# Moving thirty small on-chip DMAs from SyncE's queue to ScalarE's, behind the copy that feeds them

## The chip, the cores and the metric

The kernel runs on one core of a Trainium2 chip. A core has a matrix engine (TensorE, PE in the profile), a vector engine (VectorE, DVE), an activation engine (ScalarE, ACT), a general engine (GpSimd, POOL) and a synchronisation engine (SyncE, SP). Each works through its own list of instructions in order and waits on semaphores. DMAs are issued by an engine's instruction and carried out by 16 DMA engines. The metric is the device time of one execution in microseconds (us).

## The reference

The input x is 2 batches of 1024 tokens of width 512. Cut to what is computed:

```
xn = layernorm(x)                              # no gain, no bias
q, k, v = (xn @ W.T + b for W, b in ...)       # 32 heads of 16 values each
att = softmax(causal(q @ k.T / 4))
s   = (att @ v) @ Wo.T + bo
g   = silu(xn @ Wb.T + bb + routed low-rank delta of 8 experts, best 2)
out = x + s * g
```

Everything is float32.

## The kernel before, in words

**Units and steps.** The attention is cut into 16 units (b, oc, c): a batch b of 2, a group oc of 8 heads (4 groups), and a chunk c of 512 query tokens (2 chunks). A unit is a row of steps: 5 steps for c = 0 and 13 for c = 1 (`unit_steps`, from L1199). The plan has 144 steps. In step n TensorE makes the scores of a 128-key block against up to 512 queries for 4 heads, two of them to a score tile (`scores`, L1524, matmuls at L1538), ScalarE takes the exponential of them in two instructions, one for each score tile (`pt<-s`), GpSimd zeroes what the causal mask forbids (`masked`, L1553, L1566 in the profile; only in steps on the diagonal), and TensorE multiplies with the values (`values`, L1571, matmuls at L1590). TensorE's order is: scores of step n, values of step n - 1, then filling work of step n, then scores of step n + 1. The filling work are the projections (`q`, `p`, `pq`, `pk`, `pv`, `ph`, `po`, all matmuls at L228).

There are two score tiles a step and two buffers, so the scores of step n + 1 overwrite what the exponentials of step n read. They cannot start before these are done.

**The queries' tile.** For each unit after the first, the queries are split into a high part in a short float format (float32r) and the remainder, the low part, and both are laid out for the scores. The tile `qT` holds 128 rows and 4 planes of 512 queries. Planes 0 and 1 serve the even heads (high, low), planes 2 and 3 the odd heads. The steps are these:
- `split_queries` (L473): ScalarE writes the high part to planes 0 and 2 in one instruction (`qT<-qf`, 128x1024), VectorE subtracts and writes the low part to plane 1.
- `copy_remainder` (L478): ScalarE copies plane 1 to plane 3 (`qT<-qT`, 128x512).
- `place_queries` (L481, the DMA at L484): two DMAs inside the tile. The first copies, in planes 0 and 1, the even rows onto the odd rows; the second copies, in planes 2 and 3, the odd rows onto the even rows. Each moves 64 rows of 4096 bytes, 256 KB. Scores of the unit may start when the DMA of their planes has landed.

The keys go the same way with `place_keys` (L465), two DMAs of 128 KB for a unit.

**Who calls it.** Two units get their queries from `qk_task` (L410), the other 13 from `split` (L486). In `qk_task` the copy comes with the last but one block of the keys' projection, in `split` it is the function `remainder`, which the planner places. That makes 15 copies and 30 placing DMAs. Before the change the DMAs are issued by SyncE, whose queue also carries nearly every other transfer of the kernel: weights, x, the parts of the weights kept in DRAM, the layout change of x, the softmax denominators and the outputs.

**The planner.** All engines' orders are written out by hand (`manual_schedule`); no scheduler reorders them. A function `fill` (L1431) decides, step by step while the program is built, which small pieces come next. It keeps a guess of when VectorE and ScalarE are free (`Metered`, L40: a base price and a rate for each instruction, added to `.free`). Pieces for which a price is given in `costs` wait for a step where ScalarE has room:

```
calm = lambda more: act.free + more < begins + 0.75
...
if x[1] in costs and not calm(costs[x[1]][0]) and n < costs[x[1]][1]:
    continue
```

The first number of `costs` is the price and the second the step by which the piece goes in anyway. For `remainder` this is 3 steps ahead of the unit's first. The list `later` holds pieces for a later step, and `urgent` those that are issued at the end of a step or just ahead of the next scores (`place_urgent`, L1519).

**Semaphores of DMAs.** The program's DMAs take eight completion semaphores in turn, in the order of the program, whichever engine issues them. A DMA waits until the one that had its semaphore before it has landed.

The function that the change touches:

Of the kernel before, what the change touches and what calls it, by code (L numbers as in the profile page):

```python
# [81 lines left out]
def direct(ctx, tc, sound, x, wq, wk, wv, wo, wb, wa, wg, wB, bq, bk, bv, bo, bb, out):  # L82
# [9 lines left out]
    nc = tc.nc  # L92
    ve = Metered(nc.vector, 0.19, 966)
    act = Metered(nc.scalar, 0.22, 1274)
# [124 lines left out]
    turned_at, now = {}, [0]  # L219
    xns, xnTs, kTs, qTs, vs, gs, oTs, kfs = {}, {}, {}, {}, {}, {}, {}, []  # L220

    def mm_tile(name):
        return ps_mm.tile([P, D], F32, tag="mm", name=name)

    def matmul(o, lhsT, rhs, start, stop):

        for j in range(0, P, 32):
            nc.tensor.matmul(  # L228
                o[j : j + 32],
                lhsT=lhsT[:, j : j + 32] if len(lhsT.shape) == 2 else lhsT[:, j // 32],  # L230
                rhs=rhs,
                start=start,
                stop=stop,
            )
# [175 lines left out]
    def qk_task(b, oc, c):  # L410

        xnT = xnTs[b, c]
        qk_begun.append((b, oc, c))
        qT, kT = split_tiles(b, oc, c)
        qf = sb.tile([P, C], F32, tag="qf", bufs=2, name=f"qf_{b}_{oc}_{c}")
        kf = sb.tile([P, C], F32, tag="kf", bufs=2, name=f"kf_{b}_{oc}_{c}")
        bias_q, bias_k = (b_pair[:, n + oc : n + oc + 1] for n in (0, KC))
        pq = mm_tile("pq")
        for k in range(KC):
            matmul(  # L420
                pq, lhsT=wqks[oc][:, k, :], rhs=xnT[:, k, :], start=k == 0, stop=k == KC - 1
            )
            if k < KC - 1:
                yield MM
        act.activation(qf, pq, AF.Identity, bias=bias_q)
        split_queries(qT, qf)
        yield MM
        pk = mm_tile("pk")
        for k in range(KC):
            matmul(  # L430
                pk, lhsT=wqks[oc][:, KC + k, :], rhs=xnT[:, k, :], start=k == 0, stop=k == KC - 1
            )
            if k == KC - 2:
                copy_remainder(qT)
                later.append((now[0], lambda: place_queries(qT)))
            if k < KC - 1:
                yield MM
        if c:
            act.activation(
                kT, pk.unsqueeze(1).to_broadcast([P, 2, C]), AF.Identity, bias=bias_k  # L440
            )
            ve.tensor_scalar(kf, pk, bias_k, None, ALU.add)
            ve.tensor_tensor(kf, kf, kT[:, 0].bitcast(F32), ALU.subtract)
        else:
            act.activation(kf, pk, AF.Identity, bias=bias_k)
            split_keys(kT, kf, kf)
        later.append((now[0], lambda: place_keys(kT, kf)))
        qk_done[b, oc, c] = now[0]
        yield MM
# [8 lines left out]
    def split_keys(kT, kf, low):  # L458

        act.activation(kT, kf.unsqueeze(1).to_broadcast([P, 2, C]), AF.Copy)  # L460
        ve.tensor_tensor(low, kf, kT[:, 0].bitcast(F32), ALU.subtract)

    def place_keys(kT, low):
        for par in range(2):
            nc.sync.dma_start(out=kT[1 - par :: 2, par].bitcast(F32), in_=low[par::2])  # L465

    def split_tiles(b, oc, c):
        qT = sb.tile([P, 4, C], F32R, tag="qT", bufs=2, name=f"qT_{b}_{oc}_{c}")
        kT = sb.tile([P, 2, C], F32R, tag="kT", bufs=4, name=f"kT_{b}_{oc}_{c}")
        qTs[b, oc, c], kTs[b, oc, c] = qT, kT  # L470
        return qT, kT

    def split_queries(qT, qf):  # L473
        high = qT.rearrange("p (a h) c -> p a h c", a=2)[:, :, 0]
        act.activation(high, qf.unsqueeze(1).to_broadcast([P, 2, C]), AF.Copy)
        ve.tensor_tensor(qT[:, 1], qf, qT[:, 0].bitcast(F32), ALU.subtract)

    def copy_remainder(qT):  # L478
        act.activation(qT[:, 3], qT[:, 1].bitcast(F32), AF.Copy)

    def place_queries(qT):  # L481
        for par in range(2):
            both = qT[:, 2 * par : 2 * par + 2].bitcast(F32)
            nc.sync.dma_start(out=both[1 - par :: 2], in_=both[par::2])  # L484

    def split(b, oc, c, qf, kf):  # L486

        qT, kT = split_tiles(b, oc, c)
        split_keys(kT, kf, kf)

        def queries():
            split_queries(qT, qf)
            room["acc"] += 1
            later.append((now[0] + 1, remainder))

        def remainder():
            copy_remainder(qT)
            urgent.append((now[0], lambda: place_queries(qT)))

        by = starts[b, oc, c]  # L500
        costs[queries], costs[remainder] = (1.1, by - 4), (0.6, by - 3)
        later.append((now[0] + 1, queries))
        urgent.append((now[0] + 1, lambda: place_keys(kT, kf)))

# [264 lines left out]
    def qk_blocks_task(k):  # L769
# [36 lines left out]
        yield MM  # L806
        add(q[1], product("q4", at(1, 1)), q[1], less)
        splits.append((now[0] + 1, lambda: split(b, oc, c, qf, kf), (b, oc, c)))
        qk_done[b, oc, c] = now[0]
        ended[0] += 1  # L810
# [277 lines left out]
    turns, turned, posts, posted, later, patient, last_out = [], [], {}, [], [], [], []  # L1088
# [16 lines left out]
    bases, whole_wo, splits, costs, urgent = {}, [], [], {}, []  # L1105
# [200 lines left out]
    for b in range(NB):  # L1306
        for c in range(NC):
# [11 lines left out]
            for oc in range(KC):  # L1319
                takes = {"acc": 1}  # L1320
                if (b, oc, c) in units[1:3]:
                    Task(
                        starts[b, oc, c] - (1 if c else 2), qk_task(b, oc, c), 8 * MM, takes=takes | {"qT": 1, "kT": 1}, uses=xn, frees=takes,
                        ready=lambda u=units[units.index((b, oc, c)) - 1], t=turned_: u in qk_begun
                        and t() and (u == units[0] or now[0] >= starts[units[1]]),
                    )
                elif oc or b or c:
                    stage(
                        qk_blocks_task, ("qk", b, c, oc), starts[b, oc, c] - 5, 7 * MM, takes, xn,
                        turned_,  # L1330
                    )
# [39 lines left out]
            if (b, c) != (NB - 1, NC - 1):  # L1371
                by = min(len(plan) - 3, done + (21 if c else 22 if b else 30))
# [738 lines left out]
```

## Time and profile before

| What | Value |
|---|---|
| Time, median of 3 runs (lowest, highest) | 561.15 us (560.59, 562.68) |
| The profiled execution: its own time / its span | 560.8 us / 559.1 us |
| Granted clock of TensorE, mean | 0.993 |
| Busy: PE / DVE / ACT / POOL | 97% / 60% / 63% / 21% of the span |
| Exponentials `pt<-s` on ACT | 288, 1024 ns each, 290.2 us |
| The copies `qT<-qT` on ACT | 15, 623 ns each, 9.3 us |
| The placing DMAs on SP's queue | 30, 585 ns median each to issue |

How to read it. Busy time counts instructions that do arithmetic; a DMA's issue and a wait are not busy. An engine written with a q (SPq, ACTq) is the engine's sequencer issuing a DMA. An arrow in brackets after an idle time names what ended that idle time. A row of the timeline has the start, the duration, the engine, the line and the operation with output and input tiles; x2 means two instructions merged into one row.

### The profile page before, as it was taken

Reading aid. Unit: us, or ns where it says so; the run is one execution under the profiler, and the core shown is the slowest. Engines: PE = TensorE matmul, PEld = TensorE weight load, DVE = VectorE, ACT = ScalarE, POOL = GpSimd, SP = SyncE. Lnnn points to the kernel's source line nnn. Section 1 sums busy time; section 2 is a strip of 40 time slices with the busy share of each in tenths; the row PEclk is TensorE's granted clock in tenths of the full one; section 3 lists DMA queues with packets and bytes.
Section 4 is the critical chain, followed back from the end, with each engine's and each line's share of the span. In section 5 each row is a group of like instructions: output and inputs, shape, how many; then the busy total and the mean of one; then the engine's idle time right before and its main releaser. Section 6 shows DMA issues by size and latency. Waiting matters only on the chain.

```text
span 559.1 us, 19432 instructions
## 1 busy us (share of the span) xinstructions
PE 540.1 (97%) x8411; PEld 279.9 (50%) x8411; DVE 334.4 (60%) x693; ACT 351.5 (63%) x389; POOL 118.6 (21%) x248
## 2 busy tenths in 40 slices
PE   8999999789999999999999999999999999999994
PEld 7435444444445554454645554444545554456651
DVE  4435587266478676466559765575267553648833
ACT  2537754566677766766667756656667777776540
POOL 2213401020213431130214330130103331020500
PEclk9999999899999999999999999999999999999998
DMA  8634370686623663832555545640124221652211
GB/s 257 178 111 165 126 230 4 201 289 201 169 82 135 228 219 110 245 99 79 174 173 176 171 155 169 198 152 23 59 80 137 79 83 45 229 170 81 97 40 46
DMA packets 65198, 79.16 MB, mean 142 GB/s; under 512 B 9560, under 2 KB 52576, under 8 KB 63696
## 3 DMA queue, kind: packets, MB, share of 16 engines
q1 hardware_dynamic: 65088, 77.83, 43.4%
q8 instruction: 68, 1.11, 0.9%
q14 instruction: 26, 0.21, 0.1%
q10 hardware_dynamic: 16, 0.00, 0.0%
HBM read 46.39 MB, written 19.37 MB: 118 GB/s over the span
## 4 chain that ended last, share of the span: by engine, by line
PE 87%; DMA 5%; DVE 3%; SPq 1%; ACT 1%; issue 1%; ACTq 0%; DVEq 0%
PE av L1590 24%; PE p L228 21%; PE s L1538 17%; PE q L228 13%; PE pv L228 2%; PE po L228 2%; PE ph L228 2%; PE pq L228 1%; PE pk L228 1%; DMA qT<-qT 1%; ACT pt L56 1%; DMA back<-rc 1%; DVE x L56 1%; DMA wqk<-in_wq_dram 1%; DMA wqk<-in_wk_dram 1%; DMA gr<-kept_g 1%
## 5 line engine op out<-in xcount | busy, mean ns | idle before, releaser
L56 ACT ACTIVATE pt<-s 128x1024 f32<-128x1024 f32 x288 | 290.2, 1024 | 157.4 <-PE s L1538 149.8
L1566 POOL TENSOR_SCALAR_AFFINE_SELECT pt<-pt 128x256 f32<-128x256 f32 (+1 forms) x224 | 110.6, 509 | 414.6 <-ACT pt L56 414.0
L1590 PE MATMUL av<-pt,v 128*32 128x512 f32 (+3 forms) x1680 | 157.3, 469 | 0.2 <-DVE v L56 0.2
L1538 PE MATMUL s<-qT,kT 32*128 32x512 f32 (+3 forms) x1616 | 108.9, 364 | 6.3 <-ACT pt L56 3.8
L1538 PEld LDWEIGHTS s<-qT,kT 32*128 32x128 f32 x1616 | 62.3, 183 | 65.4 <-issue 38.7
L1590 PEld LDWEIGHTS av<-pt,v 128*32 128x32 f32 x1680 | 41.8, 109 | 54.3 <-issue 38.1
L228 PE MATMUL p<-wt,asum 128*32 128x256 f32 x960 | 58.7, 379 | 0.0
L228 PE MATMUL q<-asum,wqk 128*32 128x256 f32 x832 | 51.2, 379 | 1.7 <-DVE qf L56 1.7
L228 PEld LDWEIGHTS p<-wt,asum 128*32 128x32 f32 x960 | 31.3, 110 | 28.9 <-issue 11.7
L228 PEld LDWEIGHTS q<-asum,wqk 128*32 128x32 f32 x832 | 26.5, 110 | 26.1 <-issue 6.9
L228 PE MATMUL q<-xnT,wqk 128*32 128x256 f32 x624 | 39.5, 379 | 0.0
L56 DVE TENSOR_TENSOR g<-p,g 128x512 f32<-128x512 f32 x20 | 13.8, 689 | 26.5 <-PE p L228 26.4
L228 PEld LDWEIGHTS q<-xnT,wqk 128*32 128x32 f32 x624 | 20.2, 110 | 18.4 <-issue 6.6
L56 DVE SCALAR_TENSOR_TENSOR kf<-q,kf 128x256 f32<-128x256 f32 x39 | 16.5, 424 | 19.5 <-PE q L228 18.6
L228 PE MATMUL p<-w,xnT 128*32 128x256 f32 x448 | 28.1, 379 | 0.0
L228 PEld LDWEIGHTS p<-w,xnT 128*32 128x32 f32 x448 | 15.7, 110 | 10.3 <-issue 3.6
L228 PE MATMUL p<-w,asum 128*32 128x256 f32 x320 | 20.7, 379 | 0.0
L228 PEld LDWEIGHTS ph<-wag_sb,xnT 128*32 128x32 f32 x512 | 15.9, 114 | 4.8 <-issue 3.0
L56 DVE TENSOR_TENSOR kf<-kf,kT 128x512 f32<-128x512 f32 x15 | 10.3, 684 | 12.1 <-ACT kT L56 12.0
L228 PE MATMUL ph<-wag_sb,xnT 128*32 128x136 f32 x512 | 17.4, 287 | 0.0
L228 PE MATMUL po<-wo,oT 128*32 128x512 f32 x128 | 16.5, 593 | 0.4 <-ACT oT L56 0.4
L56 DVE TENSOR_TENSOR qT<-qf,qT 128x512 fp32r<-128x512 f32 x15 | 10.5, 699 | 10.4 <-ACT qT L56 10.4
(145 smaller groups left out, 556.3 us busy)
## 6 DMA issues: line engine op xcount, KB each, us to landing
wt<-kept SPq DMA_DIRECT2D x40, 256.0 KB
qT<-qT SPq DMA_DIRECT2D x30, 256.0 KB
x<-in_x_dram SPq DMA_DIRECT2D x16, 256.0 KB
kept<-wqk SPq DMA_DIRECT2D x4, 1024.0 KB
wqk<-kept SPq DMA_DIRECT2D x4, 1024.0 KB
kT<-kf SPq DMA_DIRECT2D x30, 128.0 KB
scr<-sq SPq DMA_DIRECT2D x6, 512.0 KB
xnT<-scr SPq DMA_DIRECT2D x24, 128.0 KB
```

Source lines behind the costliest of these rows:

```text
L56: return getattr(self.engine, name)(*args, **named)
L228: nc.tensor.matmul(o[j : j + 32], lhsT=lhsT[:, j : j + 32] if len(lhsT.shape) == 2 else lhsT[:, j // 32], rhs=rhs, start=start, stop=stop,)
L1538: nc.tensor.matmul(ss[s // 2][:, s % 2, col : col + w], lhsT=keys[rows, kt % TT * P : kt % TT * P + P], rhs=q[rows, halves * par + half_, ...
L1566: nc.gpsimd.affine_select(out=d, in_=d, compare_op=ALU.is_ge, fill=0.0, base=0, pattern=[[0, d.shape[1]], [1, P]], channel_multiplier=-1,)
L1590: nc.tensor.matmul(avs_now[par][32 * s : 32 * s + 32, q0 : q0 + w], lhsT=vs[b, kt][:, h * VS - HD * par : h * VS - HD * par + HP], rhs=pt[ ...
```

## The change

The two placing DMAs are issued by ScalarE in place of SyncE, directly behind ScalarE's copy of the remainder, in both callers. They no longer go through `later` or `urgent`. The planner's guess of ScalarE's free time is raised by 0.55 for each of the two DMAs, and the price of `remainder` goes from 0.6 to 1.7. Its last step stays the same.

```diff
             if k == KC - 2:
                 copy_remainder(qT)
-                later.append((now[0], lambda: place_queries(qT)))
+                place_queries(qT)
...
     def place_queries(qT):
         for par in range(2):
             both = qT[:, 2 * par : 2 * par + 2].bitcast(F32)
-            nc.sync.dma_start(out=both[1 - par :: 2], in_=both[par::2])
+            nc.scalar.dma_start(out=both[1 - par :: 2], in_=both[par::2])
+            act.free = max(act.free, act.ready) + 0.55
...
         def remainder():
             copy_remainder(qT)
-            urgent.append((now[0], lambda: place_queries(qT)))
+            place_queries(qT)

         by = starts[b, oc, c]
-        costs[queries], costs[remainder] = (1.1, by - 4), (0.6, by - 3)
+        costs[queries], costs[remainder] = (1.1, by - 4), (1.7, by - 3)
```

## The prediction, on record before the changed kernel had run

> **What bounds the kernel now.** I began with the page: is there an engine without idle time?
>
> ```profile
> PE 540.1 (97%) x8411; PEld 279.9 (50%) x8411; DVE 334.4 (60%) x693; ACT 351.5 (63%) x389; POOL 118.6 (21%) x248
> ```
>
> TensorE is busy for 540.1 of 559.1 us. The change adds no matmul, and the changed program has all 11459 instructions of TensorE in the old order. So it can only act through TensorE's 19 us of idle time: the first 2.5 us, some 9 us at the tail, and a few stalls between. TensorE's own waits name those that a score matmul suffers (columns: total us, times, longest):
>
> ```profile
> PE s L1538 <- ACT pt L56: 3.8, 3, 2.8
> PE s L1538 <- DMA qT<-qT: 2.3, 1, 2.3
> ```
>
> One placement of thirty stalls TensorE, for 2.3 us. That is the most this part can give. The groups show how much room ScalarE has:
>
> ```profile
> L56 ACT ACTIVATE pt<-s 128x1024 f32<-128x1024 f32 x288 | 290.2, 1024 | 157.4 <-PE s L1538 149.8
> ```
>
> Of 157.4 us idle ahead of the exponentials, 149.8 end with TensorE's scores. ScalarE normally waits for TensorE, not the reverse. What an issue costs a sequencer, SyncE's placements first (minimum, median, maximum ns), then the only two DMAs that ScalarE issues now:
>
> ```profile
> L484 SPq DMA_DIRECT2D qT<-qT x30: 464/585/1354, 39.3 to 493.8; - x30
> ```
>
> ```profile
> L152 ACTq DMA_DIRECT2D b_rows<-in_bq_dram x1: 550/550/550, 0.8 to 0.8; - x1
> L153 ACTq DMA_DIRECT2D b_rows<-in_bk_dram x1: 259/259/259, 1.4 to 1.4; - x1
> ```
>
> Then the timeline around all 15 copies. The common place, ScalarE alone:
>
> ```profile
> 163.09 0.62 ACT L56 ACTIVATE qT<-qT 128x512 fp32r<-128x512 f32 x1
> 164.63 2.02 ACT L56 ACTIVATE pt<-s 128x1024 f32<-128x1024 f32 x2 [0.91 <-PE s L1538]
> ```
>
> The copy ends at 163.72 and the next exponentials start 0.91 us later. The first of the tight places:
>
> ```profile
> 38.65 0.63 ACT L56 ACTIVATE qT<-qT 128x512 fp32r<-128x512 f32 x1 [0.76 <-DVE qT L56]
> ...
> 41.23 1.92 ACT L56 ACTIVATE pt<-s 128x1024 f32<-128x1024 f32 x2
> ...
> 43.21 1.15 PE L1538 MATMUL s<-qT,kf 32*128 32x256 f32 x16
> ```
>
> Here no idle time stands before the exponentials, and the scores start 0.05 us after these end. The last place is the tightest: copy and exponentials follow without a gap, and TensorE is already waiting for ScalarE:
>
> ```profile
> 493.13 1.92 ACT L56 ACTIVATE pt<-s 128x1024 f32<-128x1024 f32 x2
> 493.25 1.11 SPq L484 DMA_DIRECT2D qT<-qT  x2
> ...
> 495.10 0.74 PE L1538 MATMUL s<-qT,kT 32*128 32x256 f32 x14 [0.53 <-ACT pt L56]
> ```
>
> And the one stall that a placement makes:
>
> ```profile
> 118.87 6.50 DMA qT<-qT
> 125.37 0.14 issue
> 125.51 0.74 PE s L1538 x6
> ```
>
> These are pieces of the chain that ended last. The copy was done at 115.87; SyncE came to the placement 3.0 us later, behind weight loads, and it landed 6.5 us after that.
>
> [...] the pair issued from 118.87 took its sequencer 1.86 us, its first half 6.50 us to land. [...] SyncE would save 30 x 0.585 = 17.6 us, but SyncE isn't the bound. [...]
>
> **The change part by part.** *ScalarE's new work.* The first DMA waits for ScalarE's own copy, 0.03 us (SyncE starts 0.03 after a copy ends). The pair takes 1.10 to 1.19 us on SyncE where undisturbed; I take 1.15. With 0.07 to the next activation, ScalarE is ready 1.25 us after the copy's end. Bounds for the pair: 0.55 (twice ScalarE's cheaper issue) and 2.5 (twice SyncE's dearest, nearly).
>
> *What is queued behind it* is the next exponential, and behind that TensorE's next scores, which need the score tiles free. At 38.65 the key activations stand between: they start at 40.53, not 39.55, and the exponentials end at 44.14, not 43.16. TensorE loses 0.95. At 492.61 the exponentials start at 494.47, not 493.13: lost 1.3, all of it, since TensorE already waits. At 434.62 (ScalarE did a tanh just before) idle is 0.40: late by 0.85, against 0.51 from the exponentials' end to the scores; lost 0.4, and 0.1 more at the mask behind. At 451.21 late by 0.33 against 0.08: lost 0.3. Sum 3.05.
>
> At the common place it is late by 0.34: 1.25 less 0.91. Scores follow the exponentials' end by 0.53, so these hide it; the masked tiles that the values read are finished 0.38 ahead (167.48 against 167.86), so about nothing is left. Nine places like this I price at 0.4 together. Two (305.50, 354.99) have 1.6 to 1.8 us and cost nothing.
>
> *SyncE's issues in the same moment.* In five common places SyncE itself issues then (at 180.88, 197.20, 288.82, 324.24, 416.06). [...] half an issue more each time, with no cover left: 0.2 x 4, 0.8 in sum. Nothing to 3 are the bounds.
>
> *Waits for semaphores.* Each DMA on ScalarE now also waits for the one that last had its completion semaphore. I looked up all thirty in the old trace: each had landed by then, the nearest at 197.11 against 198.39 (a store of the layout change). Cost nothing; the cover is 1.3 us there, and everything beyond goes to the exponentials.
>
> *Copies moved.* The dearer price pushes five copies 1 to 7 steps later, to 2 steps ahead of their unit. From there some 7 us pass until the first scores; an undisturbed pair lands in 2.9 (163.74 to 166.67). Hidden, with 4 us left. The copy of weights `wqk` near 46 goes one step later; idle time covers it. SyncE's later transfers come 1.2 us sooner, and no TensorE stall waits for one.
>
> *The gain.* At 115.9 the placement no longer waits for SyncE. What is late next is ScalarE: its copy of `wqk` waited 2.01 us for a weight load, ran from 120.74, and the exponentials behind it ended at 123.85. Scores cannot start before 123.9: at most 1.6 of 2.34 is won. And the placement now moves 512 KB while that load is under way, 1.25 us at the 410 GB/s of 120 to 122; the engines were 0.74, 0.92 and 0.50 busy from 115 to 118, so about half of it fits: load late by 0.6[...]. Gain 0.9, bounds 0 and 2.3.
>
> *Sum.* 3.05 + 0.4 + 0.8 - 0.9 = 3.35 on the profiled execution: span 562.4, its own time 560.8 + 3.35 = 564.15. The median of the runs is 561.15, 0.35 above that execution. I say 564.3, which is 0.56% over the median. A measurement of this kernel can tell about 0.5% from no change, that is 558.3 and 564.0.
>
> **The rivals.** *Main case*, as above: chance 0.45, own range 562.8 to 566, about 0.27 of it above 564.0.
>
> *Hidden for the most part*: the pair costs ScalarE 0.8 us. Then 0.6 + 0.95 + 0.15 are lost and the rest is covered; less a gain of 1.0, 561.85. For it: 149.8 us of waiting for TensorE, and 0.26 for ScalarE's second issue. Against it: that issue moved 4 rows, these move 64, and SyncE needs 0.59 for each second one. Chance 0.27.
>
> *Not slower*: [...] the pair takes 0.55, so only 0.35 and 0.7 are lost: 559.9. It decides from where the pair's price falls under 0.95, at which the two losses are about the gain. Against it: the exponentials that end at 123.85. Chance 0.12, 0.04 of it below 558.3.
>
> *ScalarE held by the shared machinery*: [...] With the cover spent, eleven places pay in full, 5.5: 568 with a smaller gain. For it: SyncE's issues reach 1.35 and 1.43 us in the crowded stretch at 115 to 122. Against it: outside that they keep under 0.6. Chance 0.16.
>
> **How the numbers follow.** Slower: 0.27 + 0.16 = 0.43. Same: 0.18 + 0.27 + 0.08 = 0.53. Faster: 0.04. The range 560.9 to 567.5 leaves out most of the third case (0.08) and the upper part of the fourth (0.10).
>
> **What would show it.** Right: thirty issues on ACTq of 0.5 to 0.6 us, ScalarE's wait for scores down by some 17 us, TensorE waiting for `pt` some 3 us longer with entries near 44, 436 and 496, and no wait for `qT<-qT`. The stall at 123 to 125 shrinks to 1 to 2 us and is then put down to ScalarE. Wrong: issues of 0.3 us on ACTq, a step after a copy without lateness, a placement that stalls TensorE elsewhere, or ScalarE waiting for a DMA ahead of an issue.

## The result

| | before | after |
|---|---|---|
| Median (lowest to highest) | 561.83 us (560.59 to 562.68), 4 runs | 568.04 us (566.49 to 572.07), 4 runs |
| After / before | | 1.0129, 95% interval 1.0085 to 1.0174 |
| Profiled execution: span, mean clock | 559.1 us, 0.993 | 566.5 us, 0.991 |

The change makes the kernel 1.3% slower by the ratio; the medians are 6.2 us apart. 3.35 us were forecast. When both were run again it was 567.2 us against 560.49, ratio 1.0109 (1.0067 to 1.0151). A ratio in this document need not be the quotient of the medians beside it.

First the page, TensorE's row:

```profile
PE 545.7 (96%) x8411; PEld 285.2 (50%) x8411; DVE 334.6 (59%) x693; ACT 350.4 (62%) x389; POOL 117.7 (21%) x248
```

No matmul was added and TensorE is busy 5.6 us longer. The prediction had said that the change can act only through idle time. Two things make busy time grow: a lower clock (below), and ends of matmuls that the profile models, so that a matmul held up half way looks long (the step that is 0.97 us late at 44 shows only 0.21 us of waiting, below). TensorE's waits alone therefore don't give the loss:

```profile
PE s L1539 <- ACT pt L56: 6.5, 8, 2.2
PE q L228 <- DVE qf L56: 3.9, 2, 3.3
```

They were 3.8 for ScalarE and 1.7 for VectorE; the 2.3 us for `qT<-qT` is gone. ScalarE's side, the exponentials and the issues:

```profile
L56 ACT ACTIVATE pt<-s 128x1024 f32<-128x1024 f32 x288 | 289.2, 1024 | 162.9 <-PE s L1539 150.9
```

```profile
L484 ACTq DMA_DIRECT2D qT<-qT x30: 472/572/1089, 39.7 to 499.1; - x30
```

An issue on ScalarE's queue costs what it cost SyncE: median 572 ns against 585. Yet the idle time ahead of the exponentials did not fall by 17 us, it is 150.9 after 149.8. The idle column counts the issue as idle time, so it doesn't show how much of a wait a sequencer's work has used up.

A better ruler than waits, since TensorE's order is the same in both: the end of each step's second exponential, after minus before, from the two traces. Below this is called the lateness. It moves in few places (stretches of steps that move it by less than 0.02 us have no row):

| Where (steps) | changed, first profile | changed, second | queue alone |
|---|---|---|---|
| Start, before the first placement | 0.41 | 0.17 | 0.15 |
| 3 (copy at 39) | 0.97 | 0.96 | 0.97 |
| 4 to 17 | 0.11 | 0.15 | 0.01 |
| 18 to 25 (the stall at 123) | 0.42 | -0.49 | -0.86 |
| 33 to 36 (copy at 165) | 0.62 | 0.86 | 0.66 |
| 37 to 94 | 0.05 | 1.27 | 0.60 |
| 95 | 2.08 | 3.42 | -1.14 |
| 111 to 115 (copy at 439) | 0.41 | 0.42 | 0.41 |
| 116 to 128 (copy at 456) | 0.26 | 0.24 | 0.24 |
| 129 (copy at 498) | 1.31 | 1.32 | 1.32 |
| 130, 131 | 1.24 | 1.21 | 1.38 |
| 132 to 143 | 0.17 | 0.21 | -0.01 |
| Sum, and the tail behind it | 8.05, -0.62 | 9.71, -0.41 | 3.73, -0.51 |

The last column is an experiment below. In the first two, sum and tail give the spans' differences, 7.4 and 9.3 us. How good is the ruler? A second profile of the kernel before differs from the first by at most 0.07 us in every row but one: at steps 18 to 25 it is 1.98 us later. In that row lie the stall at 123 and, in the kernel before, a stretch at half clock (107 to 111), so single profiles don't give its size.

The tight places look as forecast; here is the first, in the timeline (start, duration, engine):

```profile
39.72 1.17 ACTq L484 DMA_DIRECT2D qT<-qT  x2
...
42.62 1.92 ACT L56 ACTIVATE pt<-s 128x1024 f32<-128x1024 f32 x2
...
44.59 0.50 PE L1539 MATMUL s<-qT,kf 32*128 32x256 f32 x4 [0.21 <-ACT pt L56]
```

Issue, key activations and exponentials follow one another, the exponentials start at 42.62 where they started at 41.23 (0.41 us of that arose before the copy), and TensorE waits for them.

Three losses have no term in the prediction's sum. The first stands behind the tightest place, in the timeline:

```profile
498.58 1.12 ACTq L484 DMA_DIRECT2D qT<-qT  x2
...
499.75 1.94 ACT L56 ACTIVATE pt<-s 128x1024 f32<-128x1024 f32 x2 [1.20 <-PE p L228]
...
500.83 0.39 PE L1539 MATMUL s<-qT,kT 32*128 32x256 f32 x2 [1.41 <-ACT pt L56]
...
501.74 0.86 PE L1539 MATMUL s<-qT,kT 32*128 32x256 f32 x14 [0.53 <-ACT pt L56]
```

The exponentials follow the issue, and TensorE waits 1.41 us and then 0.53. Then, busy time in three stretches of 3.4 us (length, TensorE's busy time and matmuls, granted clock, DMA share, GB/s):

```profile
498.80:502.20 3.40, 1.47 (x26) 1.00 0.87 294
502.20:505.60 3.40, 3.40 (x42) 0.50 0.03 10
505.60:509.00 3.40, 3.40 (x68) 1.00 0.00 0
```

For 3.4 us the clock is granted at half, and 42 matmuls are done where the next stretch does 68. That is the 1.24 us at steps 130 and 131. It lasts 3413 ns, as the stretch at 126.74 in this profile does, and the tail's begins at 563.64: the three starts lie 110.01 and 18.00 times 3413 ns apart, so on one grid. I laid windows of 3413 ns along TensorE's busy time in 16 profiles, on the grid that the half-clock stretches give, and counted those at full clock from 7 us after the start to 7 us before the last half-clock stretch, that of the tail. After all 18 windows with a busy share of 0.43 or less the next ran at half, though several were far from idle; between 0.44 and 0.63 it followed in 4 of 16; above that, never. Three of the stretches lasted two windows, though TensorE was 0.88 to 0.90 busy in the first of them; the count leaves these out and doesn't explain them.

The second is at step 95. In the chain that ended last:

```profile
371.05 6.02 DMA gr<-kept_g
...
378.58 2.08 DVE asum L56 x2
...
381.10 1.93 PE q L228 x32
```

A load that VectorE needs lands 6.02 us after its issue began (4.53 before), and TensorE waits 3.27 us for VectorE in place of 1.09. Two additions behind it take 2.08 us together where they took 1.20, so 0.9 us of the loss may be theirs; what slows them wasn't tried.

The third is the pair at 165:

```profile
165.94 1.60 ACTq L484 DMA_DIRECT2D qT<-qT  x2
...
167.59 1.94 ACT L56 ACTIVATE pt<-s 128x1024 f32<-128x1024 f32 x2 [1.68 <-PE av L1591]
```

Its second issue took 1.09 us. Both are taken up after the experiments.

And the gain at 123 to 125 that was forecast as 0.9:

```profile
116.96 5.51 DMA wqk<-in_wk_dram
...
123.84 1.83 ACT pt L56 x2
...
125.71 0.73 PE s L1539 x3
```

The placement is off the path and the weights' load is what ScalarE waits for, as forecast; TensorE waits 0.84 and 0.41 us there, not 2.34. But two stalls of 0.28 and 0.53 come before, the window was 0.63 busy, and the half clock that the kernel before had at 107 to 111 came at 127 to 130 instead.

Whether a placement that ScalarE issues is spared SyncE's backlog was open before the change had run. The queues, before and after:

```profile
q10 hardware_dynamic: 16, 0.00, 0.0%
q10 hardware_dynamic: 2416, 7.87, 3.7%
```

The thirty placements went over to q10. The one at 117 was issued 0.03 us after its copy in place of 3.0. But from the start of the issue to the end of its last packet 6.3 us passed, and before the change 6.50 us to the landing of its first half. What was saved there is the wait ahead of the issue; that the landing itself became much faster isn't shown.

### The profile page after: what moved, and what is told of

It is laid out like the page before. It is cut to its first block, busy times and chain, and to the rows that moved or that the text cites. A ratio compares the mean times of both kernels' runs of the same rounds, so it can differ in the third digit from the quotient of the medians.

```text
span 566.5 us, 19430 instructions
## 1 busy us (share of the span) xinstructions
PE 545.7 (96%) x8411; PEld 285.2 (50%) x8411; DVE 334.6 (59%) x693; ACT 350.4 (62%) x389; POOL 117.7 (21%) x248
## 3 DMA queue, kind: packets, MB, share of 16 engines
q8 instruction: 68, 1.11, 0.8%
## 4 chain that ended last, share of the span: by engine, by line
PE 87%; DMA 4%; DVE 3%; ACT 2%; issue 2%; SPq 1%; ACTq 0%; POOL 0%; POOLq 0%; DVEq 0%
PE av L1591 23%; PE p L228 21%; PE s L1539 17%; PE q L228 12%; PE po L228 2%; PE pv L228 2%; PE ph L228 2%; ACT pt L56 2%; PE pq L228 1%; PE pk L228 1%; DMA gr<-kept_g 1%; DMA wqk<-in_wk_dram 1%; PE warm L183 1%; DMA back<-rc 1%; DVE x L56 1%
## 5 line engine op out<-in xcount | busy, mean ns | idle before, releaser
L56 ACT ACTIVATE pt<-s 128x1024 f32<-128x1024 f32 x288 | 289.2, 1024 | 162.9 <-PE s L1539 150.9
L1539 PE MATMUL s<-qT,kT 32*128 32x512 f32 (+3 forms) x1616 | 110.9, 365 | 6.5 <-ACT pt L56 6.3
L1591 PEld LDWEIGHTS av<-pt,v 128*32 128x32 f32 x1680 | 43.1, 109 | 54.2 <-issue 37.8
L228 PE MATMUL p<-wt,asum 128*32 128x256 f32 x960 | 60.2, 385 | 0.3 <-DMA wt<-kept 0.3
L228 PEld LDWEIGHTS p<-wt,asum 128*32 128x32 f32 x960 | 33.1, 112 | 29.3 <-issue 12.4
L56 DVE TENSOR_TENSOR x<-p,x 128x512 f32<-128x512 f32 x15 | 10.3, 687 | 10.5 <-PE p L228 10.5
```

The lines of the kernel that those rows point to most:

```text
L56: return getattr(self.engine, name)(*args, **named)
L228: nc.tensor.matmul(o[j : j + 32], lhsT=lhsT[:, j : j + 32] if len(lhsT.shape) == 2 else lhsT[:, j // 32], rhs=rhs, start=start, stop=stop,)
L1539: nc.tensor.matmul(ss[s // 2][:, s % 2, col : col + w], lhsT=keys[rows, kt % TT * P : kt % TT * P + P], rhs=q[rows, halves * par + half_, ...
L1591: nc.tensor.matmul(avs_now[par][32 * s : 32 * s + 32, q0 : q0 + w], lhsT=vs[b, kt][:, h * VS - HD * par : h * VS - HD * par + HP], rhs=pt[ ...
```

## The experiments

Four theories. Theory 1: the loss is ScalarE's time just ahead of exponentials that have no slack. Theory 2: it is the planner's new order. Theory 3: it is chance of one execution, or the DMAs' own path. Theory 4, formed on the way: an issue costs ScalarE time only because it waits for the copy just ahead of it.

| Kernel | Median, us | Before, run beside it | Ratio (95%) |
|---|---|---|---|
| changed, again | 567.2 | 560.49 | 1.0109 (1.0067 to 1.0151) |
| order alone | 560.65 | 560.49 | 0.9998 (0.9984 to 1.0012) |
| queue alone | 565.41 | 560.49 | 1.0077 (1.0052 to 1.0101) |
| ScalarE's time without DMAs | 565.57 | 560.3 | 1.0102 (1.0079 to 1.0125) |
| four tight units on SyncE | 562.55 | 560.3 | 1.0042 (1.0025 to 1.0059) |
| half of each pair | 563.67 | 560.3 | 1.0046 (1.003 to 1.0061) |
| stalled unit only | 560.12 | 560.3 | 0.999 (0.997 to 1.001) |
| queue, last unit on SyncE | 562.84 | 560.52 | 1.0049 (1.0034 to 1.0065) |
| queue, tight units behind | 561.47 | 560.52 | 1.0023 (1.0007 to 1.0038) |
| order, and stalled unit | 560.46 | 560.52 | 1.0003 (0.9991 to 1.0016) |
| queue, all behind | 561.72 | 560.81 | 1.0015 (0.9998 to 1.0032) |
| changed, all behind | 562.93 | 560.81 | 1.0034 (1.0016 to 1.0051) |

### What recurs

The two kernels unedited, for second profiles.

> A second profile of the kernel before, to see which of its stalls recur. Theory 1 (the loss is ScalarE's time at the few places without slack) needs a steady kernel before: no wait of TensorE for ScalarE near 44, 436 and 452, and 0.5 us near 495, as in the first profile; span 559 within 1. Theory 3 (the large single losses of the changed kernel, 2.08 us at 378 and 1.2 us at half clock behind 502, are chance of one execution) expects the stall for VectorE near 376 (1.09 us in the first profile) and the stretch at half clock (107.3 to 110.6) to differ here by 1 us or more.

> A second profile of the changed kernel, against which to read the step-by-step lateness of the first (0.97 us at step 3, 0.62 at steps 33 to 36, 2.08 at step 95, 0.40 at steps 111 to 113, 0.24 at step 116, 2.54 at steps 129 to 131). Theory 1 (ScalarE's time): 0.97, 0.40, 0.24 and 1.3 of the 2.54 recur within 0.1. Theory 3 (chance of one execution): the 2.08 at step 95, the 0.62 at step 33 and the 1.2 at half clock don't all recur, and the time is 564 to 566 then; if all recur, 567 to 568.5 and theory 3 falls.

The kernel before, run once, came out at 563.02 us, a span of 561.3: the stall at 377 is the same (1.09 us), that at 123 is 2.86 us in place of 2.34, and a second stretch at half clock stands at 127 to 131. That one costs 1.47 us at step 24, two thirds of the difference of 2.2. The changed kernel's tight places recur to 0.02 us. So do the loss at step 33, the one at step 95 and the half clock behind 502, and the time is 567.2: the part of theory 3 that calls them chance of one execution falls for the changed kernel. New is 1.2 us near step 70, where an issue of the pair took 1.44 us.

### Order or queue

```diff
 order alone (the changed kernel, but)
-            nc.scalar.dma_start(out=both[1 - par :: 2], in_=both[par::2])
+            nc.sync.dma_start(out=both[1 - par :: 2], in_=both[par::2])
 queue alone (the changed kernel, but)
-            act.free = max(act.free, act.ready) + 0.55
-        costs[queries], costs[remainder] = (1.1, by - 4), (1.7, by - 3)
+        costs[queries], costs[remainder] = (1.1, by - 4), (0.6, by - 3)
```

> The planner's part alone: prices, five later copies and the place in the program as in the changed kernel, but SyncE issues the thirty DMAs. Theory 1 (ScalarE's time): within 1.5 us of before (560.5 to 563), no wait of TensorE for ScalarE near 44, 436, 452. Theory 2 (the later copies and the changed order cost the time): 565 to 568, and the stalls of the changed kernel at 378 and 499 are here too.

> The queue alone: ScalarE issues the thirty DMAs directly behind its copies, but the planner's prices are the old ones, so that every engine's other instructions keep the order of before. Theory 1 (ScalarE's time): 565 to 569, as slow as the changed kernel, with the same lateness at steps 3 (0.97), 111 (0.40), 116 (0.24) and 129 (1.3). Theory 2 (the later copies and the changed order): 561 to 563.

> A second profile of the queue alone. Theory 1: steps 3, 111, 116 and 129 lose 0.97, 0.40, 0.2 and 1.3 again, and one issue of the pair at step 33 takes 1.0 us or more again. The half clock at 498 depends on where the stall falls in a window, and need not recur. The stall at step 95 is absent again if it goes with the order of the changed kernel, and may be there if it is chance.

The order alone costs nothing that can be measured: 0.9998 (0.9984 to 1.0012). Theory 2 falls. The queue alone, with every engine's other instructions in the order of before, costs 0.8%, with the same lateness at the same steps. The second profile of it (565.02 us, one run) repeats steps 3 (0.97), 111 (0.42), 116 (0.24) and 129 (1.31), the slow issue at step 33 (0.91 us) and the half clock behind the last place. Neither profile has the long stall at step 95, which both profiles of the changed kernel have.

### ScalarE's time, without the DMAs

On the order alone, each copy is repeated twice:

```diff
     def place_queries(qT):
+        for again in range(2):
+            nc.scalar.activation(qT[:, 3], qT[:, 1].bitcast(F32), AF.Copy)
```

> SyncE issues the thirty DMAs, in the order of the changed kernel, but ScalarE repeats each of the fifteen copies twice more, some 1.1 to 1.2 us of arithmetic in place of the pair of issues. Theory 1 (the loss is ScalarE's time ahead of the next exponentials, whatever takes it): the lateness of the changed kernel without a DMA on ScalarE's queue: 0.9 to 1.0 at step 3, 0.3 to 0.5 at steps 111 to 113, 1.2 to 1.4 at step 129 with a stretch at half clock behind it, 563.5 to 566 against 560.65 for the order alone. Theory 3 (the DMAs' own path: issue, second queue, landing): 560 to 562, none of these.

```profile
39.71 1.29 ACT L483 ACTIVATE qT<-qT 128x512 fp32r<-128x512 f32 x2
...
44.55 0.71 PE L1541 MATMUL s<-qT,kf 32*128 32x256 f32 x8 [0.21 <-ACT pt L56]
```

The arithmetic stands where the issues stood, and TensorE waits the same 0.21 us at 44.6. The lateness is 0.94 at step 3, 0.38 over steps 111 to 113 and 1.32 at step 129. So at the tight places it is ScalarE's time, whatever takes it, and not the queue. The half clock, which had been expected, did not follow: the stall at 497 to 499 fell into two windows, 0.63 and 0.80 busy, and steps 130 and 131 lost nothing, where the four profiles with that stall inside one window (0.43 busy: the changed kernel and the queue alone, twice each) lost 1.21 to 1.38. Some of this kernel's time has another source: SyncE issues 1.2 us later, and TensorE waits 3.1 us for placements. So that its total, 565.57, lies in the range of theory 1 is in part luck; the steps are the evidence.

### Taking the tight places out

```diff
 four tight units on SyncE (on the changed kernel)
+        tight = any(qTs.get(u) is qT for u in ((0, 1, 0), (1, 3, 0), (1, 2, 1), (1, 3, 1)))
-            nc.scalar.dma_start(out=both[1 - par :: 2], in_=both[par::2])
+            (nc.sync if tight else nc.scalar).dma_start(out=both[1 - par :: 2], in_=both[par::2])
 last unit on SyncE (on the queue alone)
+            on = nc.sync if qTs.get((1, 3, 1)) is qT else nc.scalar
+            on.dma_start(out=both[1 - par :: 2], in_=both[par::2])
 half of each pair (on the queue alone)
+            (nc.sync if par else nc.scalar).dma_start(out=both[1 - par :: 2], in_=both[par::2])
```

> The changed kernel with four of the fifteen units (those placed at 39, 439, 457 and 499) given back to SyncE; eleven stay on ScalarE and the order is the changed kernel's. Theory 1: 0.97 + 0.40 + 0.24 + 1.3 + 1.3 at half clock are gone, so 562.5 to 564 from 567.2; what stays is some 0.6 at step 33 and 2 to 3.4 at step 95. Theory 3 (many ScalarE issues each cost a little): 4 of 15 of the loss goes, so 565 to 566.

> The queue alone, with the last unit of fifteen (placed at 492 in the kernel before) given back to SyncE; the other fourteen stay on ScalarE. Theory 1 without the clock: only the 1.3 us at step 129 goes, 564.1 from 565.4. Theory 1 with the clock (the stall leaves its window of 3.4 us too idle and the next one runs at half): 2.0 to 2.7 go, 562.7 to 563.4. That the last unit matters no more than others: 565.

> ScalarE issues only the first DMA of each pair and SyncE the second, with every engine's order as in the kernel before. ScalarE is held for 0.5 to 0.6 us in place of 1.1 to 1.2. Theory 1: step 3 loses 0.4, step 129 0.7, steps 111 and 116 nothing, [...]: 561 to 562.5. If the loss came with the change of queue and not with ScalarE's time, half the gap of the queue alone or more stays: 563 to 565.

Without four units of fifteen the changed kernel's 567.2 falls to 562.55, 4.7 us of 6.7. Their own lateness and the half clock behind the last are 4.2 us of that in the changed kernel's profile, and all of it is gone; the stall at step 95 was also smaller (0.72 us). Without the last unit the queue alone falls from 565.41 to 562.84. The ratios, 1.0077 and 1.0049, lie only 1.6 us apart, with intervals that overlap, so the runs leave open how much this one unit carries. The profiles are clearer: steps 129 to 131 lose nothing now, where the queue alone lost 1.32 and, at half clock, 1.38. About half of what this unit cost there was the clock. Half of a pair loses 0.33 at step 3 and 0.69 at step 129, as theory 1 says, and no half clock stands behind it; the window with the stall was 0.72 busy. Its median is 1.2 us above what was expected and inside the range of the other reading, so the total decides nothing. Its profile has the excess in one place: 2.35 us at step 95, a stall of 1.91 and a half clock behind it.

### The same issues at another place in ScalarE's order

On the queue alone, the pair of a tight unit is kept back until the next step's two exponentials have been issued; then the same for all but the two units (placed at 63 and 115) that have no step to spare, and for the changed kernel:

```diff
     def place_queries(qT):
+        if any(qTs.get(u) is qT for u in ((0, 1, 0), (1, 3, 0), (1, 2, 1), (1, 3, 1))):
+            behind.append(qT)
+        else:
+            place_now(qT)
...
             pts.append(pt)
+        while behind:
+            place_now(behind.pop())
         return pts
```

> The queue alone, with ScalarE still issuing all thirty DMAs, but for the four tight units it issues them behind the next step's two exponentials in place of ahead of them. Theory 1 (the place in ScalarE's order decides, not ScalarE's total time): nothing is lost at step 3, 0.4 or less at each of steps 112, 117 and 130, and no half clock near 500: 561 to 562.5. If ScalarE's time as such or the change of queue is what costs: 565 as in the queue alone. If the pair then lands too late for the unit's first scores (it has some 3.4 us): waits of TensorE for the placements near 458 and 499, 563 to 565.

> ScalarE issues all thirty DMAs, in the order of the kernel before; thirteen units' pairs stand behind the next step's two exponentials, and the two without a step to spare (placed at 63 and 115) directly behind the copy. In the run with four units moved so, the issue of the pair ran while the exponentials did. Theory 4 (an issue costs ScalarE time only because it waits for the copy just ahead of it; behind two queued exponentials it runs beside them): the 0.5 us at steps 33 to 36 goes too, no loss at steps 3, 111, 116, 129, 559.5 to 561.2. If an issue of about 1 us holds the next work wherever it stands: 561.5 or more, with losses one step later than in the queue alone.

> The changed kernel (its prices, order and queue) with the same thirteen pairs behind the next step's exponentials. Theory 4: the losses at steps 3, 33, 111, 116 and 129 and the half clock near 502 go; what is left against before is the stall at step 95 that came in the three profiles with this order and ScalarE's queue: 560 to 563, and 560 to 561 if that stall goes with the time at which the DMA of the stored gate meets a 16 KB packet of the instruction queue.

The kernel with four units kept back, around the last of them:

```profile
493.59 0.61 ACT L56 ACTIVATE qT<-qT 128x512 fp32r<-128x512 f32 x1
494.11 1.00 ACT L56 ACTIVATE pt<-s 128x1024 f32<-128x1024 f32 x1
494.23 1.12 ACTq L492 DMA_DIRECT2D qT<-qT  x2
495.01 1.01 ACT L56 ACTIVATE pt<-s 128x1024 f32<-128x1024 f32 x1
```

The pair of issues, 1.12 us as ever, runs while the exponentials do. The second exponential starts at 495.01, before the pair is out at 495.35, so ScalarE's sequencer had handed it over by then; the copy ended at 494.20, so the DMA's wait is over, and the issue costs ScalarE nothing. Directly behind the copy it is different: in the changed kernel each pair starts 0.03 us after the copy's end, and the next activation only 0.05 to 0.10 us after the pair is out. No step of the four loses anything now, and with all thirteen kept back none of steps 3, 33, 111, 116 and 129 does. That is theory 4. All behind is 1.0015 (0.9998 to 1.0032), not to be told from before, though ScalarE issues all thirty. Its median is 0.5 us above the expected range and just inside the other reading's; but that reading wanted losses one step later, and the profile has none, only 0.74 us at step 95. The changed kernel so mended gives 562.93, 4.3 us under 567.2; of the 2.94 us that its profile is late at step 143, 2.73 arise at step 95. It also loses 0.3 at steps 117 and 118, where one issue of a pair kept back took 1.82 us; so a long issue (below) can cost something there too.

### Is there a faster version

Only the placement that stalled TensorE goes to ScalarE, on the kernel before and on the order alone:

```diff
 stalled unit only (on the kernel before)
+            if (b, oc, c) == (0, 1, 1):
+                place_queries(qT, nc.scalar)
+            else:
+                urgent.append((now[0], lambda: place_queries(qT)))
```

> The kernel before with one unit of fifteen changed: only the placement that stalls TensorE at 123 to 125 is issued by ScalarE. Theory 1: no tight place is touched, and the lateness between steps 17 and 25 falls by 0.9 as in the queue alone (1.13 to 0.27), so 559 to 560.3 against 560.5 before. If the stall only passes from the placement to ScalarE's copy of the weights with nothing won: 560.3 to 561.5.

> The two parts that lost nothing put together: the changed kernel's prices and order, SyncE for fourteen units, ScalarE for the one whose placement stalled TensorE at 123 to 125. Theory 1: the 0.9 of that stall and the 1.09 that the order alone saved at step 95 add up: 559 to 560.2. If neither part is more than noise: 560.2 to 561.

In the first, steps 18 to 25 gain 0.35 us where 0.9 had been expected; its ratio is 0.999 (0.997 to 1.001), the second's 1.0003. For the second 559 to 560.2 had been expected: its profile has the shortest span of all, 557.0 us, without any half clock before the tail, but over the runs the two savings don't show. No version beats the kernel before by what can be measured.

### The long issues

In every profile some issues take about 1 us or more in place of 0.5. On ScalarE's queue they go with one line of the page:

```profile
q8 instruction: 68, 1.11, 0.8%
```

68 packets of 16 KB each (1.11 MB over 68), one about every 8 us, each for 0.88 to 1.90 us in the traces of before and after, 1.08 and 1.06 in the median. "Instruction" is the kind that the profile gives this queue; what the packets are for isn't shown. Over the 16 profiles, ScalarE made 45 of its 279 placement issues while such a packet was under way; 15 of them took over 0.8 us, up to 2.16. Of the 234 others none did. On SyncE's queue the split is not as clean: 225 of 875 issues that met a packet took over 0.8 us, and 86 of 4766 that met none, so a packet isn't the only thing that goes with a long issue there. At step 95, on SyncE's queue, the split is complete. In six profiles (changed, changed again, four tight units on SyncE, half pair, and both with all behind) the packet began 0.15 to 0.34 us ahead of the issue of `gr<-kept_g`: the issue took 1.10 to 1.29 us, landed 4.87 to 6.02 us after it began, and TensorE waited 1.91 to 3.27 us there. In the ten others the packet began 0.34 to 0.99 us behind it: 0.46 or 0.47 us, landed in 3.74 to 4.57, and TensorE waited 1.09 us at most. So a shift of half a microsecond goes with 1 to 3 us. That the packet causes the long issue is what this speaks for; it is not shown, since no run took the packet away.

## Why the prediction was wrong

**The pair and the tight places: right.** ScalarE was forecast to be ready 1.25 us after the copy's end. Pairs took 1.12 us in the median, and ScalarE went on 1.20 to 1.31 us after the copy (0.03 wait, 1.12 to 1.19, 0.05 to 0.10), the long issues apart. The four losses, forecast as 0.95, 1.3, 0.5 and 0.3, were 0.97, 1.31, 0.41 and 0.26.

**The common places and SyncE's issues beside them: wrong terms.** They were priced at 0.4 and 0.8; the half issue more behind the 0.8 was the author's estimate, and no trace had shown it. Exponentials are up to 0.3 us late there for a step and in time again at the next; outside steps 33 to 36 nothing stays. Pairs during which SyncE issues too take 1.13 us, the others 1.12, and but for the long issues none takes over 1.19, so a SyncE issue at the same moment goes with 0.07 us more at most here. (The 0.8 is also 0.2 for four places, though it names five.) The 0.62 at steps 33 to 36 goes with a long issue. The second profile has one more, at step 70.

**The gain at 123: wrong size.** The mechanism held, ScalarE's weights are late next. Forecast 0.9 (1.6, less 0.6 for the late load, less 0.1 of the author's for exponentials held up by SyncE's issues, which no trace had shown); measured at steps 18 to 25: a loss of 0.42 and a gain of 0.49 in the changed kernel's profiles, gains of 0.86 and 0.10 in those of the queue alone, 0.35 with that unit alone. Taking a stall apart also moves it against the windows of 3413 ns (the half clock came at 127 in place of 107 in the changed kernel's first profile), which this term left out; how much of the scatter that is wasn't separated.

**The step that failed** is the first, "it can only act through TensorE's 19 us of idle time", with what followed from it: terms put at nothing. Where a stall left its window 0.43 busy or less, the next ran at half clock, 18 times of 18. The loss of 1.3 at 492 was priced as 1.3 and brought 1.24 more. Then "SyncE's later transfers come 1.2 us sooner, and no TensorE stall waits for one" misread the trace of before, whose chain of work has

```profile
368.46 4.53 DMA gr<-kept_g
374.78 1.20 DVE asum L56 x2
376.43 1.93 PE q L228 x32
```

TensorE already waited 1.09 us there for VectorE, which had waited 2.41 us for that load of SyncE's. So there was no slack, and when the load landed after 6.02 us and the additions took 2.08, step 95 lost 2.08 us. The load's issue met a 16 KB packet in that profile and not in the one of before; that this is the reason stays open. With the 0.62 of the long issue at 165 that is 3.94 us which no term held. The forecast of 3.35, less 1.2 for common places and SyncE's issues, plus 1.3 for the gain that failed, 0.7 spread over the other rows (0.41 of it ahead of the first placement) and 3.94 is 8.1, against 8.05 found at step 143.

**The rivals.** 568 is what "ScalarE held by the shared machinery" named, but its 0.5 us more for each pair was the author's estimate and isn't what was measured: 0.07 at most with SyncE issuing, 0.03 from the copy to the pair, and not eleven places paying in full. Of its picture only the long issue is real, at one or two pairs of fifteen. So 568 is right by luck, and its own terms (3.05 and 5.5, less at most 0.9) give 568.8 or more. "Hidden for the most part" needed a pair of 0.8 us and "not slower" one under 0.95; pairs took 1.12. "Not slower" had also taken all of the 2.34 us at 125 as won, which nothing had shown; it fails on the exponentials at 123, as argued.

**The signs to look for.** Thirty issues of 0.5 to 0.6 us (but for one of 1.09), TensorE's waits for `pt` some 3 us longer (6.5 after 3.8), none for `qT<-qT`, and at 123 to 125 a stall of 1.25 us put down to ScalarE: seen. ScalarE's wait for scores down by 17 us: not seen, since the idle column holds the issue time itself.

## What to carry to other kernels

A DMA issued directly behind the instruction that feeds it waited here for that instruction's end, and what was queued behind started later by the whole issue, 1.12 us for a pair; where there is no slack, that is lost. Moved behind work that is ready to run, the same issues cost nothing in these profiles, but for 0.3 us at one long issue. Price a stall of the engine that bounds the kernel at its own length and, if it can leave a clock window (3413 ns here) 0.43 busy or less, at a further 1.2 to 1.4 us, as measured here. Ask of each stall of that engine what the engine that it waits for was itself waiting for. Where two engines' timing is within half a microsecond of a collision, compare several profiles before giving a loss to the edit.

## What was not expected of the hardware

- The half clock needs no idle window: a busy share of 0.43 in 3413 ns was enough every time, 18 of 18, and the next 3413 ns ran at 0.50.
- ScalarE's sequencer issued a DMA (494.23 to 495.35) while its engine worked on exponentials handed over earlier (494.11 to 496.02).
- An issue on ScalarE that met a 16 KB packet of the instruction queue took up to 2.16 us in place of 0.5; without one, none of 234 went over 0.8. Which of the two brings the other about wasn't tried.
- Times spread from run to run: 562.0 to 569.4 in 14 runs of the queue alone, 559.5 to 561.7 in 14 of the order alone, 559.7 to 564.3 in 27 of the kernel before run beside them, but 559.1 to 567.6 in 53 of it run beside later ones.
